# A selective scan in two tiles: one scan instruction over both, with a zero decay between them

## The chip, the cores and the metric

The kernel runs on one core of a Trainium2 chip. The metric is the device time of one execution in microseconds (us); lower is better. Engines are named as in the profile: PE is the matrix engine, DVE the vector engine, ACT the scalar engine, POOL GpSimd, and SP the engine that issues most plain DMAs.

## The reference

Eight samples of 256 channels and 1024 tokens pass through two layers. The first is a Mamba block: layer norm, a projection to 512 inner channels, a short causal convolution, a selective state-space scan, a gate, a projection back, and a feed-forward part. The second is full attention over the 1024 tokens with eight heads, followed by a mixture of experts of which two out of eight are used for each sample. Everything is fp32.

The part that the change touches is the scan. For each inner channel `d` and each of 16 states `s` it computes, token by token:

```python
dA = jnp.exp(dt_t[..., None] * A)
h = dA * h + (dt_t * x_t)[..., None] * B_t[:, None, :]
y = jnp.einsum('bds,bs->bd', h, C_t)
```

`h` begins at zero for each sample. There are 512 x 16 independent recurrences of 1024 tokens per sample.

## The kernel before

**Tiling.** The tokens of a sample are cut into two chunks of `CH` = 512. The 512 inner channels lie in four tiles of 128 partitions, taken in two halves of two tiles each (`NHALF` = 2). A step is one chunk, one state `s` and one half `h`: its tile `hb` has 128 partitions, two channel tiles `q` and 512 tokens. There are 16 chunks of 32 steps (`NSTEP`), so 512 steps. Steps with an even chunk number are those of a sample's first chunk; they start the recurrence from 0. Those with an odd number start from `state`, a small tile in which the last token of each row of the first chunk was put.

**One step.** Five functions, called by the loop over `now` near line 1606, make it up:

- `decay(g, q)` (line 568): one ACT exponential, `dt` times `-A`, into a 128x512 tile `da`, for tile `q`. `da` has four buffers, so that the decays of step `now + 2` are written where those of step `now` were read.
- `inputs(g)` (line 578): one DVE product, 128x1024, of `xd` with the broadcast row `B_t`, into `hb`.
- `scan(g, q)` (line 589): one DVE scan instruction per tile `q`, in place in `hb`. In the last call of a first chunk a POOL copy puts the last column of both tiles into `state`.
- `sums(g)` (line 604): one DVE product of `hb` with the row `C_t`, and a POOL DMA that adds the result to the accumulator of the chunk.
- `load_bc` (line 555): one SP DMA, 512 KB, which brings both rows of a state, broadcast over the partitions; it is used by the two halves.

**Order.** The order in the loop is scan 0, decay 0 of `now + 2`, scan 1, decay 1 of `now + 2`, `inputs` of `now + 1`, `sums` of `now`. The product of the next step thus stands between the scan and the sums that read it, and the sums stand between that product and the scan that reads it.

All other work is written as generators: `prologue` (norm, projection, convolution, `dt` for the next chunk), `gate_part`, `epilogue` (gate, projection, feed-forward of the chunk that has ended), `attention`, `project_part` and `experts`. A planner in the kernel (`Model`, `Queue`, `advance`, lines 62 to 119 and 1529 to 1549) keeps an estimate of when each engine is free. After each piece of a step it calls `advance`, which lets the generators issue their next instructions until the estimated time has caught up with DVE. A DVE instruction is charged as follows, and ACT and PE in a similar way:

```python
    def vec_cost(op, out, *_):
        return 0.16 + width(out) * (2.08e-3 if op == "tensor_tensor_scan" else 1.04e-3)
```

What the planner decides is only the order of the instructions on each engine; the synchronisation is by semaphores. An attention can begin when the `epilogue` of its sample's second chunk has ended, and its experts when the attention has been projected. After the last step, `while due: idle(0.25)` issues what is left.

Of the kernel before, what the change touches and what calls it, by code (L numbers as in the profile page):

```python
# [17 lines left out]
P = 128  # L18
# [36 lines left out]
def hybrid_kernel(ctx: ExitStack, tc: tile.TileContext, a: dict, out: bass.AP):  # L55
# [79 lines left out]
    def V(name, i=None, n=1):  # L135
        lo, hi = VEC[name]
        return vecs[:, lo:hi] if i is None else vecs[:, lo + i : lo + i + n]
# [297 lines left out]
    def prologue(i: int):  # L435
# [104 lines left out]
        for h in range(NHALF):  # L540
            dx = yield from mem.take(f"dx_{i}_{h}")
            dxs.append(dx)
            for r in range(2):
                act.activation(dx[:, r, :], xm[h][:, r, :], AF.Identity, scale=V("D", 2 * h + r))
        for h in range(NHALF):
            yield max(landed[h], model.end)
            vec.tensor_tensor(xm[h], xm[h], dts[h], ALU.mult)
        mem.end()
        me["acc", 0], me["acc", 1] = dxs
        me["xd"], me["dt"] = xm, dts  # L550


    das, bcs, hbs = {}, {}, {}

    def load_bc(n):
        i, s = divmod(n, NS)
# [6 lines left out]
    def place(g):  # L563
        i, k = divmod(g, NSTEP)
        s, h = divmod(k, NHALF)
        return i, s, h

    def decay(g, q):
        i, s, h = place(g)
        da = work_pool.tile([P, CH], F32, name=f"da_{g}_{q}", tag="da", bufs=4)  # L570
        n = (2 * h + q) * NS + s
        act.activation(da, chunk[i]["dt"][h][:, q, :], AF.Exp, scale=neg_a[:, n : n + 1])
        das[g, q] = (da, act.at)
        if q and s == NS - 1:
            model.end = act.at
            t4.put(chunk[i]["dt"][h])

    def inputs(g):

        i, s, h = place(g)  # L580
        hb = hbs[g] = h4.now(f"hb_{g}")
        bc, landed = bcs[g // NHALF]
        vec.at = max(vec.at, landed)
        xd = chunk[i]["xd"][h]
        vec.tensor_tensor(hb, xd, bc[:, 0, :].unsqueeze(1).to_broadcast([P, 2, CH]), ALU.mult)
        if s == NS - 1:
            t4.put(xd)

    def scan(g, q):

        i, s, h = place(g)
        c = i % NCH
        hb = hbs[g]
        d = 2 * h + q
        da, done = das.pop((g, q))
        vec.at = max(vec.at, done)
        vec.tensor_tensor_scan(
            hb[:, q, :], da, hb[:, q, :], 0.0 if c == 0 else state[:, s, d : d + 1],
            ALU.mult, ALU.add,
        )  # L600
        if q and c < NCH - 1:
            pool.tensor_copy(state[:, s, 2 * h : 2 * h + 2], hb[:, :, CH - 1])

    def sums(g):
# [891 lines left out]
    with tc.tile_pool(name="work", bufs=1) as work_pool:  # L1496

        def tagged(tag, n):
            return Slots(
                lambda nm, k: work_pool.tile([P, 2, CH], F32, name=nm, tag=f"{tag}_{k}"), n  # L1500
            )

        t4, h4, pt4 = tagged("t4", T4), tagged("h4", H4), tagged("pt", PT)
        for b in range(B):
            for m, nm in ((x1_d, "x1_d"), (t_d, "t_d"), (xf_d, "xf_d")):
                m[b] = dram.tile([NCH, P, KC, CH], F32, name=f"{nm}_{b}", tag=f"{nm}_{b}")

        class Scratch:


            def __init__(self, slots):
                self.slots, self.k, self.tile = slots, 0, work_pool.tile

            def keep(self, n, name, shape, dtype):
                return work_pool.tile(shape, dtype, name=name, tag=f"t4_{self.slots[n]}")

            def tmp(self, name, shape, dtype):
                self.k = (self.k + 1) % (len(self.slots) - 3)
                return self.keep(3 + self.k, name, shape, dtype)

        due, done = [], set()
        URGENT = {"a": 0, "p": 1, "g": 2, "e": 2, "o": 3, "s": 4, "x": 5, "y": 5}

        def start(stream, key, at=0.0):
            due.append([at, URGENT[key[0]], len(done) + len(due), stream, key])

        def advance():


            while True:
                model.t = min(model.t + TICK, vec.at)
                for d in sorted(due, key=lambda d: d[1:3]):
                    while d in due and d[0] <= model.t + 0.05:
                        if d[1] > 2 and max(pe.at, act.at) > model.t + LAG:
                            break
                        model.end = model.t
                        try:
                            at = next(d[3])  # L1540
                        except StopIteration:
                            due.remove(d)
                            done.add(d[4])
                            break
                        if at == POLL:
                            break
                        d[0] = (model.end if at is None else at) + 0.1
                if model.t >= vec.at:
                    break

        def idle(t):

            vec.at += t
            advance()

        def heads_and_projections():
            for b in range(B):
                while ("e", b * NCH + NCH - 1) not in done or ("s",) not in done:
                    yield POLL
                yield from attention(b)  # L1560

        def setup():
            mem = Owner(t4, 8)
            tiles = []
            for n in range(8):
                tiles.append((yield from mem.take(f"setup_{n}")))
            held = []
            for n in range(2):
                held.append((yield from pairs.take(f"setup_p{n}")))
            pl = Scratch([t4.of[id(t)][1] for t in tiles])  # L1570
            yield from fold(w1, HID // P, "ln2_g", "ln2_b", b1, "b1")
            yield
            yield from column_bias(pl)
            yield
            yield from bounds(pl)
            yield
            yield from values_bias(pl)
            expert_constants(pl)
            mem.put(*tiles)
            mem.end()  # L1580
            pairs.put(*held)

        def all_experts():
            for b in range(B):
                while not all(("o", b, c) in done for c in range(NCH)):
                    yield POLL
                yield from experts(b)

        first = prologue(0)
        next(first)  # L1590
        for t, src in loads:
            nc.sync.dma_start(t, src)
        run(fold(w_in, 2 * ND, "ln1_g", "ln1_b", b_in, "b_in"))
        start(first, ("p", 0))
        while ("p", 0) not in done:
            idle(0.25)
        start(heads_and_projections(), ("a",))
        start(all_experts(), ("x",))
        start(setup(), ("s",))
        nsteps = B * NCH * NSTEP  # L1600
        for n in range(AHEAD):
            load_bc(n)
        for n in range(4):
            decay(n // 2, n % 2)
        inputs(0)
        for now in range(nsteps):
            i, k = divmod(now, NSTEP)
            if k == FRONT and i + 1 < B * NCH:
                start(prologue(i + 1), ("p", i + 1), model.t)
            if k == GATE:  # L1610
                start(gate_part(i), ("g", i), model.t)
            n = now // NHALF + AHEAD
            if now % NHALF == 0 and n < B * NCH * NS:
                while "bc_d" not in chunk.get(n // NS, {}):
                    idle(0.5)
                load_bc(n)
            if now + 2 < nsteps:
                while "dt" not in chunk.get((now + 2) // NSTEP, {}):
                    idle(0.5)
            for q in range(2):  # L1620
                scan(now, q)
                advance()
                if now + 2 < nsteps:
                    decay(now + 2, q)
            if now + 1 < nsteps:
                while not h4.free:
                    idle(0.5)
                inputs(now + 1)
                advance()
            sums(now)  # L1630
            if k == NSTEP - 1:
                start(epilogue(i), ("e", i), model.t)
            advance()
        while due:
            idle(0.25)

        mx = work_pool.tile([P, 1], F32, name="mx", tag="s_mx")
        vec.tensor_reduce(mx, loads_e, AX.X, ALU.max)
        vec.tensor_scalar(mx, mx, capacity / L, None, ALU.is_gt)
        vec.tensor_tensor(bad, bad, mx, ALU.max)  # L1640
        vec.tensor_copy(flag, bad[0:1, :])
# [255 lines left out]
```

## Time and profile before

| | us |
|---|---|
| median of 3 runs | 3751.08 |
| lowest and highest | 3748.72, 3759.55 |
| profiled execution, its own time | 3752.05 |
| span of the profiled execution | 3750.2 |
| busy PE, DVE, ACT, POOL | 2954.9, 3127.6, 2519.5, 953.3 |
| first scan starts | 77.9 |
| last scan starts | 3297.4 |

The profile is one execution. A group of instructions is shown with its count, its busy time (overlaps counted once), its mean duration in ns, and the idle time of the engine just before it with what ended it. In a timeline a row has the start in us, the time that the merged instructions cover, and the engine; start minus start is what an instruction occupies when the next follows at once. A row of a table by stretches has the stretch, its length, and then the busy time and the count for PE, PEld (the weight loads), DVE, ACT and POOL, and at last the granted PE clock, the DMA share and GB/s. The mean granted PE clock of the execution is 0.882. All instructions but DMA issues are recorded by one helper, so that they carry one line number (L100) and are told apart by their tiles.

### The profile page before, as it was taken

The page shows a single profiled execution, that of the slowest core. Times are in us where ns is not written, and L with a number is a line of the kernel's source. Part 1 is how long each engine was busy: PE and PEld are TensorE (multiplying, and loading weights), DVE is VectorE, ACT ScalarE, POOL GpSimd, SP SyncE. Part 2 cuts the span into 40 slices and gives each one's busy share as a digit, 9 for nine tenths or more (in the row PEclk, how much of TensorE's full clock was granted, in tenths as well). Part 3 has the DMA queues.
Part 4 walks back from the last instruction along what each step waited for, and adds up shares of the span by engine and source line. Part 5 has one row for each costly group of instructions (what it writes and reads, how often), then busy time and mean ns, then how long its engine had stood idle before and what let it go on. Part 6 is the DMA issues. An engine that isn't in the chain of part 4 may idle for free. (4 is left out here: it accounts for less than half of the span.)

```text
span 3750.2 us, 33234 instructions
## 1 busy us (share of the span) xinstructions
PE 2954.9 (79%) x11155; PEld 1084.8 (29%) x11155; DVE 3127.6 (83%) x3322; ACT 2519.5 (67%) x3437; POOL 953.3 (25%) x1046
## 2 busy tenths in 40 slices
PE   4312636788788897988888987989898988999976
PEld 2101212322333223323233323332332323333322
DVE  4969999999899999997999899989999899932021
ACT  4333636687667876777868785877778795865644
POOL 0133123312341234322332223222322342211010
PEclk7655767899889998989899998989899999999988
DMA  4347787778687978887887878887878897832030
GB/s 113 69 92 175 161 176 173 169 164 176 159 205 164 207 159 191 199 195 163 179 194 164 196 169 186 196 181 175 191 174 179 200 204 170 200 84 82 34 76 21
DMA packets 178853, 596.84 MB, mean 159 GB/s; under 512 B 25184, under 2 KB 27872, under 8 KB 178672
## 3 DMA queue, kind: packets, MB, share of 16 engines
q0 software_dynamic: 103392, 364.44, 49.9%
q1 hardware_dynamic: 75280, 230.18, 19.0%
q8 instruction: 90, 1.47, 0.2%
q14 instruction: 91, 0.75, 0.1%
HBM read 234.36 MB, written 58.20 MB: 78 GB/s over the span
## 5 line engine op out<-in xcount | busy, mean ns | idle before, releaser
L100 ACT ACTIVATE da<-dt,neg_a 128x512 f32<-128x512 f32 x1024 | 721.2, 718 | 631.9 <-DVE hb L100 621.7
L95 POOL DMA_DIRECT2D dx<-hb x512 | 443.3, 867 | 1692.2 <-DVE hb L100 1440.8
L100 DVE TENSOR_TENSOR hb<-hb,bc 128x1024 f32<-128x1024 f32 x512 | 625.7, 1222 | 34.0 <-POOL state L100 20.2
L100 DVE TENSOR_TENSOR_SCAN hb<-da,state,hb 128x512 f32<-128x512 f32 x512 | 632.3, 1272 | 9.1 <-ACT da L100 9.1
L100 DVE TENSOR_TENSOR hb<-xm,bc 128x1024 f32<-128x1024 f32 x512 | 616.7, 1204 | 11.2 <-DMA dx<-hb 11.1
L100 DVE TENSOR_TENSOR_SCAN hb<-da,hb 128x512 f32<-128x512 f32 x512 | 603.9, 1211 | 1.0 <-ACT da L100 0.9
L100 ACT ACTIVATE pt<-sc 128x1024 f32<-128x1024 f32 x512 | 493.8, 1016 | 57.4 <-PE sc L100 57.1
L100 PE MATMUL sc<-qk,qk 32*128 32x512 f32 x2048 | 365.4, 665 | 57.9 <-ACT pt L100 43.2
L100 POOL COPY state<-hb 128x2 f32<-128x2 f32 x256 | 241.9, 945 | 454.8 <-DVE hb L100 450.9
L100 PE MATMUL num<-pt,v 128*32 128x512 f32 x2048 | 288.2, 632 | 46.4 <-DVE ot L100 46.4
L100 PE MATMUL facc<-fh,w 128*128 128x512 f32 x512 | 254.0, 647 | 35.0 <-ACT fh L100 22.2
L100 PE MATMUL den<-pt,ecb 128*32 128x512 f32 x2048 | 279.5, 614 | 0.0
L100 PE MATMUL fh<-x_f,w 128*128 128x512 f32 x480 | 239.2, 629 | 9.2 <-ACT fh L100 5.0
L100 PE MATMUL re<-he,g 128*128 128x512 f32 x472 | 223.1, 618 | 18.3 <-ACT he L100 10.1
L100 PE MATMUL he<-xe,g 128*128 128x512 f32 x448 | 221.1, 619 | 9.5 <-DVE fo L100 6.2
L100 ACT ACT_TABLE_LOAD x171 | 219.4, 1283 | 6.7 <-PE var_a L100 3.0
L100 PE MATMUL mo<-sz,w_out 128*128 128x512 f32 x256 | 125.6, 636 | 102.5 <-DVE sz L100 102.2
L100 PEld LDWEIGHTS sc<-qk,qk 32*128 32x128 f32 x2048 | 106.8, 188 | 290.8 <-ACT pt L100 114.0
L100 PE MATMUL z<-xz,w_in 128*128 128x512 f32 x256 | 130.0, 641 | 45.8 <-DMA xz<-xn_d 31.5
L100 PE MATMUL xin<-xn,w_in 128*128 128x512 f32 x256 | 134.6, 659 | 32.2 <-DVE xn L100 21.0
L100 PEld LDWEIGHTS facc<-fh,w 128*128 128x128 f32 x512 | 103.4, 208 | 186.6 <-issue 135.1
L100 DVE SCALAR_TENSOR_TENSOR xm<-xp,vecs,xm 128x512 f32<-128x512 f32 x192 | 143.4, 748 | 12.8 <-ACT xm L100 8.2
(320 smaller groups left out, 3922.7 us busy)
## 6 DMA issues: line engine op xcount, KB each, us to landing
dx<-hb POOLq DMA_DIRECT2D x512, 512.0 KB, 6.5
bc<-bc_d SPq DMA_DIRECT2D x256, 512.0 KB, 4.4
dt<-e POOLq DMA_DIRECT2D x32, 512.0 KB, 6.1
dt<-u POOLq DMA_DIRECT2D x32, 512.0 KB, 8.7
xe<-xf_d SPq DMA_DIRECT2D x28, 512.0 KB, 6.1
xn<-in_x SPq DMA_DIRECT2D x16, 512.0 KB, 6.2
xn_d<-xn SPq DMA_DIRECT2D x16, 512.0 KB, 2.8
xz<-xn_d SPq DMA_DIRECT2D x16, 512.0 KB, 8.6
```

Of the source, the lines that this page charges most:

```text
L95: f(*args, **kw)
L100: return f(*args, **kw)
```

## The change

The decays of a step are put into one tile of two rows, `das[n]`, allocated twice for even and odd steps. The first column of its second row is set to zero once and never written again, since the second exponential starts at column 1. One scan instruction runs over the 1024 elements of both rows. Where it passes into the second row, the zero decay drops what the first row left, so that the second row starts from its first input alone.

In a first chunk that is right as it stands. In a second chunk the second row has to start from its state, so the missing term, first decay times `state`, is added to the first input by a DVE instruction on one column, `carry`, between `inputs` and the scan. The decays of the first token are computed once per chunk and half in the prologue, 16 states at a time, into `first`. Both decays of step `now + 2` are now issued after the whole scan of step `now`, and `advance` is called once where it was called twice.

```diff
+        if c:
+            me["first"] = work_pool.tile([P, NHALF, NS], F32, name=f"first_{i}", tag="first", bufs=1)
         for h in range(NHALF):
             yield max(landed[h], model.end)
             vec.tensor_tensor(xm[h], xm[h], dts[h], ALU.mult)
+            if c:
+                n = (2 * h + 1) * NS
+                act.activation(
+                    me["first"][:, h, :], neg_a[:, n : n + NS], AF.Exp, scale=dts[h][:, 1, 0:1]
+                )
...
-    def decay(g, q):
+    def decays(g):
         i, s, h = place(g)
-        da = work_pool.tile([P, CH], F32, name=f"da_{g}_{q}", tag="da", bufs=4)
-        n = (2 * h + q) * NS + s
-        act.activation(da, chunk[i]["dt"][h][:, q, :], AF.Exp, scale=neg_a[:, n : n + 1])
-        das[g, q] = (da, act.at)
-        if q and s == NS - 1:
+        da = das[g % 2]
+        for q in range(2):
+            n = (2 * h + q) * NS + s
+            act.activation(
+                da[:, q, q:], chunk[i]["dt"][h][:, q, q:], AF.Exp, scale=neg_a[:, n : n + 1]
+            )
+        decayed[g] = act.at
+        if s == NS - 1:
...
+    def carry(g):
+        i, s, h = place(g)
+        if i % NCH:
+            u = hbs[g][:, 1, 0:1]
+            vec.scalar_tensor_tensor(
+                u, state[:, s, 2 * h + 1 : 2 * h + 2], chunk[i]["first"][:, h, s : s + 1], u,
+                ALU.mult, ALU.add,
+            )
+
+    def scan(g):
...
+        vec.at = max(vec.at, decayed.pop(g))
+        row = hb.rearrange("p q t -> p (q t)")
         vec.tensor_tensor_scan(
-            hb[:, q, :], da, hb[:, q, :], 0.0 if c == 0 else state[:, s, d : d + 1],
-            ALU.mult, ALU.add,
+            row, das[g % 2].rearrange("p q t -> p (q t)"), row,
+            0.0 if c == 0 else state[:, s, 2 * h : 2 * h + 1], ALU.mult, ALU.add,
         )
...
+        das = [work_pool.tile([P, 2, CH], F32, name=f"da_{n}", tag=f"da_{n}") for n in range(2)]
...
-        for n in range(4):
-            decay(n // 2, n % 2)
+        for n in range(2):
+            vec.memset(das[n][:, 1, 0:1], 0.0)
+            decays(n)
...
-            for q in range(2):
-                scan(now, q)
-                advance()
-                if now + 2 < nsteps:
-                    decay(now + 2, q)
+            scan(now)
+            advance()
+            if now + 2 < nsteps:
+                decays(now + 2)
             if now + 1 < nsteps:
                 while not h4.free:
                     idle(0.5)
                 inputs(now + 1)
+                carry(now + 1)
                 advance()
             sums(now)
```

More of the change, by code (lines that the diff above doesn't have):

```diff
@@ L550, in prologue @@
         me["xd"], me["dt"] = xm, dts
-    das, bcs, hbs = {}, {}, {}
+    decayed, bcs, hbs = {}, {}, {}
     def load_bc(n):
@@ L587, in inputs @@
             t4.put(xd)
-    def scan(g, q):
+    def carry(g):
[7 more added lines that the diff above has]
+    def scan(g):
         i, s, h = place(g)
@@ L593, in scan @@
         hb = hbs[g]
-        d = 2 * h + q
-        da, done = das.pop((g, q))
-        vec.at = max(vec.at, done)
+        vec.at = max(vec.at, decayed.pop(g))
+        row = hb.rearrange("p q t -> p (q t)")
         vec.tensor_tensor_scan(
-            hb[:, q, :], da, hb[:, q, :], 0.0 if c == 0 else state[:, s, d : d + 1],
-            ALU.mult, ALU.add,
+            row, das[g % 2].rearrange("p q t -> p (q t)"), row,
+            0.0 if c == 0 else state[:, s, 2 * h : 2 * h + 1], ALU.mult, ALU.add,
         )
-        if q and c < NCH - 1:
+        if c < NCH - 1:
             pool.tensor_copy(state[:, s, 2 * h : 2 * h + 2], hb[:, :, CH - 1])
```

## The prediction

> **What bounds the kernel now.** I read the page first, then the groups of VectorE (DVE), its timeline step by step, the waits, and last the busy time of the stretch after the scans.
>
> Busy shares (part 1) and the 40 slices (part 2):
>
> ```profile
> PE 2954.9 (79%) x11155; PEld 1084.8 (29%) x11155; DVE 3127.6 (83%) x3322; ACT 2519.5 (67%) x3437; POOL 953.3 (25%) x1046
> ...
> PE   4312636788788897988888987989898988999976
> ...
> DVE  4969999999899999997999899989999899932021
> ```
>
> DVE holds slices 2 to 35 at 9 with a few dips. Then it falls to almost nothing, and PE runs at 9 until near the end. So there are two regimes: scans until 3299 us (the last scan), bound by DVE, and 451 us afterwards, bound by PE and by the dependent chain of the last sample. The two kinds of scan, and the waits between ScalarE (ACT) and DVE over the decays:
>
> ```profile
> L100 DVE TENSOR_TENSOR_SCAN hb<-da,state,hb 128x512 f32<-128x512 f32 x512 | 632.3, 1272 | 9.1 <-ACT da L100 9.1
> L100 DVE TENSOR_TENSOR_SCAN hb<-da,hb 128x512 f32<-128x512 f32 x512 | 603.9, 1211 | 1.0 <-ACT da L100 0.9
> ```
>
> ```profile
> ACT da L100 <- DVE hb L100: 621.7, 430, 9.4
> ...
> DVE hb L100 <- ACT da L100: 10.0, 8, 3.3
> ```
>
> A scan with a state pointer costs 0.06 us more than one with a constant start. ACT runs ahead of DVE: 430 times it stood at a decay until DVE had freed the buffer; the reverse happened 8 times.
>
> The mean durations are not what a step costs, because DVE instructions overlap. The timeline of DVE shows it by its starts (columns: start, union of the merged instructions):
>
> ```profile
> 3188.27 2.45 DVE L100 TENSOR_TENSOR_SCAN hb<-da,state,hb 128x512 f32<-128x512 f32 x2
> 3190.64 1.20 DVE L100 TENSOR_TENSOR hb<-xm,bc 128x1024 f32<-128x1024 f32 x1
> 3191.75 1.22 DVE L100 TENSOR_TENSOR hb<-hb,bc 128x1024 f32<-128x1024 f32 x1
> 3192.89 2.45 DVE L100 TENSOR_TENSOR_SCAN hb<-da,state,hb 128x512 f32<-128x512 f32 x2
> ```
>
> The product that takes 1.20 us is followed after 1.11 us: an instruction that does not need its forerunner starts 0.08 us before that one ends. A pair of scans occupies 3190.64 - 3188.27 = 2.37 us. Three other places give the prices that the change needs:
>
> ```profile
> 142.58 0.68 DVE L100 SCALAR_TENSOR_TENSOR val<-cnt,io_ch 128x512 f32<-128x512 f32 x1
> 143.29 1.02 DVE L100 TENSOR_REDUCE last<-val 128x32 f32<-128x512 f32 x1
> 144.24 2.31 DVE L100 SCALAR_TENSOR_TENSOR xm<-xp,vecs,xm 128x512 f32<-128x512 f32 x3
> 146.46 4.49 DVE L100 TENSOR_TENSOR oh<-hl,io_ch 128x2048 bf16<-128x2048 f32 x2
> 150.87 0.75 DVE L100 SCALAR_TENSOR_TENSOR xm<-xp,vecs,xm 128x512 f32<-128x512 f32 x1
> ```
>
> ```profile
> 1000.52 0.23 DVE L100 TENSOR_SCALAR obias<-obias,w2e 128x2 f32<-128x2 f32 x1
> 1000.66 2.33 DVE L100 TENSOR_TENSOR_SCAN hb<-da,hb 128x512 f32<-128x512 f32 x2
> 1002.91 1.20 DVE L100 TENSOR_TENSOR hb<-xm,bc 128x1024 f32<-128x1024 f32 x1
> ```
>
> The reduce reads `val` and starts 0.03 us after its end (142.58 + 0.68 = 143.26), not 0.08 before: reading one's forerunner costs about 0.12 us. A 2048-wide product takes (150.87 - 146.46) / 2 = 2.20 us. A tiny instruction with a pointer scalar takes 0.14 us (1000.52 to 1000.66). A pair of constant-start scans takes 2.25 us.
>
> [...] 512 scanned elements last 1211 ns, a 1024-wide product 1204 to 1222. So one 1024-wide scan should occupy what the 2048-wide product does. [...]
>
> **The change part by part.** There are 512 steps, 256 in first chunks (constant start) and 256 in second chunks (state pointer).
>
> - Merged scans. First chunk: 2.25 - 2.20 = 0.05 us saved. Second chunk: 2.37 - (2.20 + 0.06) = 0.11 us. Sum 12.8 + 28.2 = 41 us less DVE.
> - The carry, 256 times, stands directly behind the input product that it reads, and in the order of the built program its wait is on DVE itself. It makes that product cost its full latency (+0.12) and takes 0.14 itself: 0.26 x 256 = 67 us more. Behind it stand the sums of the step before, which do not read it, so no second stall; the scan comes after those. No row has a 1-wide pointer form of exactly this kind; between 0.07 (a tiny form without pointer) and 0.23 (no overlap behind it), plus 0.12, the bounds are 49 and 90 us. I take 67.
> - So DVE gains work: 67 - 41 = +26 us, about +0.15 us in each second-chunk step and -0.05 in each first-chunk step.
> - Decays. Same 1024 activations, 512 of them one element shorter. Both now wait for the whole scan, where the first waited for half of it, and both must be done before the next use. The second decay ends up to 0.72 us later. Counted over the timelines of ACT and DVE, in 15 of the 512 steps the second decay was not done when its pair's first scan began; adding up those shortfalls gives 14 us, and 26 if everything is 0.7 us later, against 10 us waited now. I take +8 (0 to +16). POOL's `state` copies stay 256 and keep their place behind the scan; SP's queue is untouched.
> - `first`: 16 activations of 16 columns, [...]two at a time in the prologue, hidden because ACT idles 622 us at the decays[...]. Two `memset`s: nothing that shows.
> - What moves. The planner charges a scan 2.08 ns per element and 0.16 per instruction, so it thinks each first-chunk step 0.16 us shorter and packs less other work beside the scans. In the built order, 100 of the attention's `pt` exponentials follow the last decay on ACT instead of 90, with 2 or 3 more `he` banks, 2 `re` banks, one `wo`. At the rates of the stretch 3452 to 3616 (sc, num, den together 3.3 us for two `pt`; `he` 2.0, `re` 3.7, `wo` 1.9), that is 16.5 + 5 + 7.4 + 1.9 = 31 us of PE that now comes after the scans. There PE has no room:
>
> ```profile
> 3299.00:3452.00 153.00, 145.34 (x544) 57.50 (x536) 41.62 (x83) 79.69 (x102) 14.64 (x17) 0.99 0.31 77
> 3452.00:3616.00 164.00, 162.22 (x898) 51.58 (x895) 15.67 (x23) 106.72 (x119) 8.21 (x9) 1.00 0.18 47
> 3616.00:3751.00 135.00, 84.92 (x188) 33.18 (x186) 33.20 (x75) 50.12 (x65) 12.39 (x13) 0.82 0.13 40
> ```
>
>  (Columns: length, then busy PE, PEld, DVE, ACT.) PE is 95% and 99% busy in the first two, but idle for 50 of the last 135 us, and the new order puts some `he` and `re` of sample 6 there. I take half: +15 (0 to +31).
>
> Sum: in the scans, DVE waits already for other things some 6% of the time, so I let a fifth of 26 + 8 - 2 (three DVE operations moved behind the scans) vanish: +25. With the tail's +15: +40 on the profiled 3752.05 us (span 3750.2), thus 3792; the shown median is 1 us lower: **3791**. A measurement of this kernel can tell about 0.3%, 11 us, from no change.
>
> **Rivals.**
> - Only the DVE sum arrives; the attention of sample 7 has to wait for its own layer anyway, and the backlog fills PE's gaps: 3751 + 20 = 3771 (3763 to 3776). For it: the idle 50 us. Against: 99% in the stretch before. Chance 0.19.
> - It cancels: DVE's idle takes the carries in and the tail takes the backlog, 3751 to 3762. Chance 0.13.
> - ACT becomes a partner in the bound: decays late in many steps, exponentials late behind them, PE later; 0.72 us in one step of ten is 37 us more, 3810 to 3830. Against: the 622 us ACT idles. Chance 0.13.
> - Faster: the carry starts without the stall and costs 0.14 or less. With 36 us for carries DVE gains 5 us of time, and at 0.07 us each it gains 23; if all of that reaches the end, and the tail takes no more than now, 3728 to 3746, say 3735. The sign turns at 41 / 256 = 0.16 us per carry. Against: the 0.12 us stall is seen wherever an instruction reads its forerunner. Chance 0.06.
> - The merge does not do what it says (a 1024-wide scan slower than two of 512): no reason seen; inside the heavy case.
>
> **How the numbers follow.** Main case 0.49 (3777 to 3808), with those above: slower 0.49 + 0.19 + 0.13 = 0.81, same 0.13, faster 0.06. The range 3758 to 3818 leaves out the faster case, part of the cancelled one and the far half of the heavy one.
>
> **What would show it.** DVE rows: scans 128x1024 x512, mean near 2.27 us (constant) and 2.34 (pointer); a carry group x256 near 0.22 us. In the timeline of a second chunk, product to carry 1.23 us, carry to sums 0.14, whole steps 4.77 instead of 4.62; in a first chunk 0.05 shorter. The last scan near 3325, and more than 451 us behind it. It is wrong if the carry follows the product after 1.11 us, if the wide scans start less than 2.1 us apart, or if the last scan ends before 3299.

## Result, and the profile after

| | before | after |
|---|---|---|
| median of 6 runs, us | 3753.89 | 3766.82 |
| lowest and highest | 3748.72, 3759.55 | 3763.82, 3774.25 |
| profiled execution, its own time | 3752.05 | 3766.41 |
| span of the profiled execution | 3750.2 | 3764.6 |
| last scan ends | 3298.7 | 3272.8 |
| span behind the last scan | 451.5 | 491.8 |

The changed kernel takes 1.0036 times as long, 95% interval 1.0022 to 1.0050: 13 us slower. The forecast was 3791, that is 40 us slower. The direction was right and the size three times too large. The table shows already that the two parts moved in opposite ways: the scans ended *earlier*, and the stretch behind them grew. The last three rows are of one profiled execution of each kernel; executions of one kernel differ by some 10 us.

First the page of the changed kernel, the busy shares and two rows of the slices:

```profile
PE 2970.2 (79%) x11155; PEld 1089.9 (29%) x11155; DVE 3139.2 (83%) x3068; ACT 2501.5 (66%) x3451; POOL 930.2 (25%) x1046
...
PE   4312627798888896999898987898889889999986
...
DVE  3979999999999999989999999999999979812121
```

DVE is 11.6 us busier (3127.6 before), with 254 fewer instructions. Its row of slices has fewer dips than before, and it falls a little earlier: slices 35 and 36 (counted from 1) hold 8 and 1, where before they held 9 and 3. The groups of DVE in the changed kernel (busy, mean ns, idle ahead):

```profile
L100 DVE TENSOR_TENSOR_SCAN hb<-da,state,hb 128x1024 f32<-128x1024 f32 x256 | 600.6, 2346 | 11.5 <-ACT da L100 11.5
L100 DVE TENSOR_TENSOR_SCAN hb<-da,hb 128x1024 f32<-128x1024 f32 x256 | 584.6, 2284 | 2.4 <-ACT da L100 2.3
...
L100 DVE SCALAR_TENSOR_TENSOR hb<-state,first,hb 128x1 f32<-128x1 f32 x256 | 56.2, 219 | 9.1
```

Three prices stand here as they were forecast: 2.28 and 2.35 us for the scans (2.27 and 2.34), 0.22 for the carry. The 9.1 us of idle ahead of the carries, with no releaser named, are 256 gaps of 35 ns (9.1 / 256). The 16 activations of `first` took 291 to 308 ns each:

```profile
L100 ACT ACTIVATE first<-neg_a,dt x16: 291/296/308, 196.4 to 3083.8; 128x16 f32<-128x16 f32 x16
```

The timeline of DVE, one step of a second chunk:

```profile
3199.96 2.34 DVE L100 TENSOR_TENSOR_SCAN hb<-da,state,hb 128x1024 f32<-128x1024 f32 x1
3202.22 1.20 DVE L100 TENSOR_TENSOR hb<-xm,bc 128x1024 f32<-128x1024 f32 x1
3203.46 0.22 DVE L100 SCALAR_TENSOR_TENSOR hb<-state,first,hb 128x1 f32<-128x1 f32 x1
3203.60 1.22 DVE L100 TENSOR_TENSOR hb<-hb,bc 128x1024 f32<-128x1024 f32 x1
3204.73 2.34 DVE L100 TENSOR_TENSOR_SCAN hb<-da,state,hb 128x1024 f32<-128x1024 f32 x1
```

Start to start: the scan occupies 2.26, the product ahead of the carry 1.24 (it was 1.11), the carry 0.14, the sums 1.13. The step takes 3204.73 - 3199.96 = 4.77 us, which is the forecast figure. The waits for the decays, from the table of waits:

```profile
ACT da L100 <- DVE hb L100: 552.4, 252, 12.3
...
DVE hb L100 <- ACT da L100: 13.8, 10, 4.2
```

ACT stands less often (252 times against 430), since a pair of decays now waits once. DVE stands 3.8 us longer. And the stretches behind the last scan (columns as before: length, then busy PE, PEld, DVE, ACT, POOL, and the PE clock, DMA share, GB/s):

```profile
3273.00:3449.00 176.00, 172.03 (x692) 66.66 (x682) 35.70 (x44) 97.42 (x119) 13.71 (x15) 1.00 0.28 65
3449.00:3616.00 167.00, 160.33 (x873) 49.27 (x874) 20.18 (x60) 97.08 (x112) 13.44 (x14) 0.96 0.17 48
3616.00:3765.00 149.00, 97.69 (x217) 39.77 (x215) 37.41 (x80) 62.09 (x79) 15.13 (x16) 0.84 0.19 50
```

PE is busy for 430 us of these 492; before, it was 392 of 452. So 38 us of PE work came behind the scans, the stretch is 40 longer, and PE idles there for 62 us as against 60. The free PE time at the end, which the forecast let take half of the displaced work, took none of it in this order.

### The profile page after: what moved, and what is told of

Read it like the earlier page. It is cut to its first block, busy times and chain, and to the rows that moved or that the text cites. A ratio compares the mean times of both kernels' runs of the same rounds, so it can differ in the third digit from the quotient of the medians.

```text
span 3764.6 us, 32994 instructions
## 1 busy us (share of the span) xinstructions
PE 2970.2 (79%) x11155; PEld 1089.9 (29%) x11155; DVE 3139.2 (83%) x3068; ACT 2501.5 (66%) x3451; POOL 930.2 (25%) x1046
## 4 chain that ended last, share of the span: by engine, by line
DVE 47%; PE 20%; issue 11%; ACT 9%; DMA 8%; POOL 4%; DVEq 0%; POOLq 0%; SPq 0%; ACTq 0%
DVE hb L100 34%; DMA dx<-hb 6%; DVE xm L100 3%; POOL state L100 3%; PE sc L100 2%; PE re L100 2%; PE num L100 2%; ACT L100 2%; PE fh L100 2%; PE he L100 2%; PE den L100 2%; PE facc L100 2%; ACT da L100 1%; ACT fh L100 1%; PE halves L100 1%
## 5 line engine op out<-in xcount | busy, mean ns | idle before, releaser
L100 ACT ACTIVATE da<-dt,neg_a 128x512 f32<-128x512 f32 (+1 forms) x1024 | 680.5, 714 | 560.7 <-DVE hb L100 552.4
L100 DVE TENSOR_TENSOR_SCAN hb<-da,state,hb 128x1024 f32<-128x1024 f32 x256 | 600.6, 2346 | 11.5 <-ACT da L100 11.5
L100 DVE TENSOR_TENSOR_SCAN hb<-da,hb 128x1024 f32<-128x1024 f32 x256 | 584.6, 2284 | 2.4 <-ACT da L100 2.3
L100 POOL COPY state<-hb 128x2 f32<-128x2 f32 x256 | 222.0, 867 | 354.3 <-DVE hb L100 345.4
L100 PE MATMUL den<-pt,ecb 128*32 128x512 f32 x2048 | 288.5, 632 | 0.0
```

Of the source, the lines that this page charges most:

```text
L100: return f(*args, **kw)
```

## Experiments

All runs in one table; ratios are to the kernel before, run on the same chip. *Scans* is the part of the profiled execution from the start of the first scan to the end of the last, called the scan phase below; *idle* is DVE's idle time in it, and *behind* is the time from the end of the last scan to the end of the span. These three are of one execution, which can lie 10 us off its kernel's median (`oldorder` 3758 against 3769, `joint` 3737 against 3727), so differences of a few us between them say nothing.

| kernel | median us | ratio [95%] | scans | idle | behind |
|---|---|---|---|---|---|
| before | 3754 | 1 | 3220.8 | 206.6 | 451.5 |
| after | 3766.8 | 1.0036 [1.0022, 1.0050] | 3193.3 | 170.3 | 491.8 |
| neworder | 3731.5 | 0.9938 [0.9921, 0.9954] | 3163.3 | 156.3 | 484.7 |
| oldorder | 3768.8 | 1.0039 [1.0025, 1.0053] | 3223.3 | 199.1 | 454.2 |
| nocarry | 3712.4 | 0.9883 [0.9866, 0.9899] | 3149.0 | 181.2 | 485.3 |
| nostall | 3859.6 | 1.0277 [1.0260, 1.0294] | 3291.9 | 286.4 | 487.9 |
| joint | 3727.4 | 0.9931 [0.9912, 0.9950] | 3184.6 | 175.3 | 471.1 |
| charge | 3777.5 | 1.0059 [1.0037, 1.0082] | 3226.0 | 212.3 | 472.1 |
| charge_all | 3789.5 | 1.0100 [1.0080, 1.0120] | 3224.4 | 215.4 | 482.4 |
| latedecay | 3726.7 | 0.9934 [0.9913, 0.9955] | 3159.3 | 152.1 | 485.0 |
| decays_last | 3758.8 | 1.0014 [1.0005, 1.0022] | 3233.5 | 216.1 | 445.4 |
| decays_first | 3798.1 | 1.0126 [1.0109, 1.0143] | 3240.2 | 229.4 | 485.9 |
| decays_later | 3740.3 | 0.9970 [0.9958, 0.9981] | 3218.0 | 204.1 | 435.3 |
| firstonly | 3730.6 | 0.9950 [0.9932, 0.9967] | 3196.1 | 202.0 | 453.8 |
| before_n1 | 3756.3 | 1.0008 [0.9999, 1.0017] | 3214.8 | 201.8 | 466.1 |
| before_n2 | 3780.4 | 1.0077 [1.0051, 1.0102] | 3226.6 | 214.4 | 473.9 |
| joint_n1 | 3744.8 | 0.9979 [0.9972, 0.9987] | 3213.5 | 207.1 | 457.4 |
| joint_n2 | 3748.4 | 0.9980 [0.9972, 0.9988] | 3205.2 | 200.5 | 464.9 |
| after_n1 | 3752.8 | 1.0005 [0.9991, 1.0018] | 3203.1 | 177.9 | 463.7 |
| after_n2 | 3765.9 | 1.0041 [1.0028, 1.0054] | 3196.7 | 175.5 | 490.3 |

### Instructions apart from order: neworder, oldorder, nocarry, nostall

`neworder` has the instructions of the kernel before in the order of the changed one, and the planner is charged as there: apart from the scans, the decays, the carries and `first`, the sequences of PE, ACT, DVE and POOL are the same in both traces.

```diff
+        if q == 0:
+            model.do(vec, 0.16 + 2 * CH * 2.08e-3)
+        nc.vector.tensor_tensor_scan(
...
                 scan(now, q)
-                advance()
-                if now + 2 < nsteps:
+            advance()
+            if now + 2 < nsteps:
+                for q in range(2):
                     decay(now + 2, q)
...
                 inputs(now + 1)
+                if (now + 1) // NSTEP % NCH:
+                    model.do(vec, 0.16 + 1.04e-3)
```

> The old instructions (two scans of 512 a step, four decay buffers, no carry) in exactly the order that the changed kernel has for all other work; the planner is charged as in the changed kernel. Theory A (what a step costs DVE and what the order does simply add): scan phase 3193 - 23 = 3170 us, about 490 us behind it as in the changed kernel, total 3744 (ratio 0.997). Theory B (other engines set the length of the scan phase, DVE's idle takes in what the carry costs): scan phase 3193, behind it 490, total 3767 (1.0035). Theory C (the longer stretch behind the scans came from the new instructions, not from the order): 451 us behind the scans, total below 3730 or about 3754.

`oldorder` is the reverse: the merged scan and the carry, with the charges and the calls of `advance` where the kernel before has them. It can't keep the place between the two scans: the merged scan stands where the first one stood, and both decays where the second did.

```diff
 # the decays, against the changed kernel
+        if q == 0:
+            return
         for q in range(2):
...
 # the scan, against the kernel before
-        vec.tensor_tensor_scan(
-            hb[:, q, :], da, hb[:, q, :], 0.0 if c == 0 else state[:, s, d : d + 1],
...
+        model.do(vec, 0.16 + CH * 2.08e-3)
+        if q == 0:
+            row = hb.rearrange("p q t -> p (q t)")
+            nc.vector.tensor_tensor_scan(
+                row, das[g % 2].rearrange("p q t -> p (q t)"), row,
+                0.0 if c == 0 else state[:, s, 2 * h : 2 * h + 1], ALU.mult, ALU.add,
+            )
```

> The new instructions (one scan of 1024, carry, first) in exactly the order that the kernel before has for all other work. Theory A: scan phase 3221 + 23 = 3244, behind it 451, total 3777 (ratio 1.006). Theory B: scan phase 3221, behind it 451, total 3754 (1.000). Theory C: behind the scans 490, total 3790 or more.

`nocarry` is the changed kernel with the carry's charge but not its instruction.

```diff
-            vec.scalar_tensor_tensor(
-                u, state[:, s, 2 * h + 1 : 2 * h + 2], chunk[i]["first"][:, h, s : s + 1], u,
-                ALU.mult, ALU.add,
-            )
+            model.do(vec, 0.16 + 1.04e-3)
```

> The changed kernel without the carry instruction (the second tile of each half starts a second chunk from zero), its charge in the planner kept, so that all other instructions stand in the same order. DVE is relieved of 256 x 0.257 = 66 us. Theory A: scan phase 3193 - 66 = 3127, behind it 490, total 3700 (0.986). Theory B: no more than 10 us less, 3757 or more (1.001). Half of the 66: 3734.

`nostall` makes the inputs a step earlier, so that a scan and a sum lie between the product and the carry that reads it. The planner's charge keeps its old place.

```diff
-                inputs(now + 1)
+                charge(now + 1)
                 carry(now + 1)
+                if now + 2 < nsteps:
+                    inputs(now + 2)
                 advance()
```

> The changed kernel with the input product issued one step earlier on DVE, so that a whole scan stands between it and the carry that reads it; all else in the same order. The carry then costs 0.14 instead of 0.26, 256 x 0.12 = 30 us less of DVE. Theory A: scan phase 3163, total 3737 (0.9955), below the kernel before. Theory B: 3760 to 3767. If the earlier product waits for the DMA that empties its buffer (landing 6.5 us, margin now 8 instead of 12.6 us), some of the 30 us come back as waits on dx<-hb.

**What the first three show.** Read the scan phase in the table as work plus idle. The stretches of the scan phase, rounded to whole us, show DVE's busy time as the third entry behind the length. They are, in this order, of the kernel before, `neworder`, `nocarry` and the changed kernel:

```profile
78.00:3299.00 3221.00, 2523.29 (x9431) 920.67 (x9435) 3014.33 (x3100) 2247.94 (x3101) 913.59 (x996) 0.88 0.76 174
```

```profile
80.00:3243.00 3163.00, 2470.65 (x9275) 903.28 (x9279) 3006.75 (x3096) 2225.68 (x3075) 893.15 (x989) 0.88 0.78 177
```

```profile
80.00:3229.00 3149.00, 2473.81 (x9271) 904.90 (x9271) 2967.72 (x2585) 2209.66 (x3091) 894.22 (x989) 0.88 0.78 178
```

```profile
79.00:3273.00 3194.00, 2499.94 (x9279) 911.92 (x9283) 3023.60 (x2842) 2209.87 (x3092) 883.56 (x989) 0.87 0.77 175
```

- From `neworder` to `nocarry` the scans are merged, and with them the waits of the decays: DVE's work in the scan phase falls from 3163.3 - 156.3 = 3007.0 to 3149.0 - 181.2 = 2967.8, by 39 us. The forecast was 41. But DVE's idle time grows by 25 at the same time, and the medians differ by 19 us: about half of what was saved did not reach the end.
- From `nocarry` to after only the carry comes in: ratios 0.9883 and 1.0036, 57 us for 256 carries (forecast 67). In the scan phase DVE's work grows by 55 and the carry gaps add 9, while its other idle time falls.
- From `neworder` to after both: work plus the 9 us of carry gaps is +25 us (3023.0 - 3007.0 + 9.1; forecast +26). The ratios say +0.98%, 37 us. In the old order, `oldorder` against before, they say +0.39%, 15 us. The mean of both is 26. The first comparison is the cleaner one; the second holds the moved places named above, too.
- The order alone is worth -0.62% with the old instructions (`neworder`), and nothing with the new ones (1.0036 against 1.0039). In both cases it shortens the scan phase (by 57 us from before to `neworder`, by 30 from `oldorder` to after) and lengthens what is behind (by 33 and 38).

Each of the three medians lies nearer to what theory A expected (what a step costs and what the order does add up) than to theory B.

The merging at its best, with nothing between the products, is in the timeline of `nocarry`; the product is followed after 1.13 us and not 1.24:

```profile
3102.10 1.22 DVE L100 TENSOR_TENSOR hb<-xm,bc 128x1024 f32<-128x1024 f32 x1
3103.23 1.22 DVE L100 TENSOR_TENSOR hb<-hb,bc 128x1024 f32<-128x1024 f32 x1
3104.37 2.34 DVE L100 TENSOR_TENSOR_SCAN hb<-da,state,hb 128x1024 f32<-128x1024 f32 x1
```

`nostall` took the carry away from the product that it reads, and lost more elsewhere. DVE's work in the scan phase is 17.5 us less (3023.0 to 3291.9 - 286.4 = 3005.5). In the changed kernel the sums start 83 ns before the carry ahead of them ends (median); if the 256 carries of `nostall` overlap what stands ahead of them as much, that is 21 us, an estimate that fits. But it costs 93 us more than the changed kernel (3859.6 - 3766.8): the product, made one step earlier, waits for the accumulating DMA that still reads its tile (median from issue to landing 6.5 us). From its table of waits (L597 is the product of `inputs`):

```profile
DVE hb L597 <- DMA dx<-hb: 162.9, 95, 6.9
```

In the changed kernel that wait is 8.5 us, 4 times. So a product made a whole step earlier is too early for the four `hb` buffers there are, and what the stall costs at the end of the kernel wasn't measured. Other places for the carry were not tried.

### Which part of the order: joint, charge, charge_all, latedecay

`joint` is the kernel before with one `advance` for both scans, and both decays behind it; charges as before.

```diff
                 scan(now, q)
-                advance()
-                if now + 2 < nsteps:
+            advance()
+            if now + 2 < nsteps:
+                for q in range(2):
                     decay(now + 2, q)
```

> The kernel before with one edit: both scans of a step in a row, then one advance, then both decays; charges as before. Theory J (what made the new order faster is that scans and decays stand together): 3735 or less. Theory K (it is the 0.16 us less that the planner charges for a first-chunk step): no change, 3750 to 3760. Theory N (any change of order moves the time by some 20 us either way, without a trend): anywhere from 3730 to 3775.

`charge` is the kernel before whose planner takes the first chunk's second scan to be 0.16 us shorter, as the changed kernel's does; `charge_all` does it in every step.

```diff
-        vec.tensor_tensor_scan(
+        model.do(vec, CH * 2.08e-3 + (0.0 if q and c == 0 else 0.16))
+        nc.vector.tensor_tensor_scan(
```

> The kernel before with one edit: in first-chunk steps the planner charges the second scan 0.16 us less, as it does for the merged scan; the instructions and the places of scans and decays stay. Theory K: 3732, with 480 to 490 us behind the last scan. Theory J: 3755. Theory N: anywhere from 3730 to 3775.

> The kernel before, the planner charging every step 0.16 us less, in second chunks too. Theory K: the scan phase shortens further (below 3163), the stretch behind it grows further (above 490), total 3715 to 3730. Theory J: 3755. Theory N: anywhere from 3730 to 3775.

`latedecay` is `neworder` with the second tile's decay issued ahead of the first's, so that both wait for both scans, as in the changed kernel.

```diff
-        n = (2 * h + q) * NS + s
...
+        for q in (1, 0):
+            n = (2 * h + q) * NS + s
```

> The run neworder (old instructions in the changed kernel's order) with one edit: of the two decays of a step the second tile's is issued first, so that on ACT both wait for the whole pair of scans, as both decays do behind the merged scan. nocarry against neworder gained 19 us where 43 us of scan occupancy were taken away. Theory L (24 us of it are lost because the decays start only when the whole scan has ended): 3731 + 24 = 3755, with DVE waits on da of 20 us or more. Otherwise: 3731.

**The charge** alone costs 0.59% and puts 21 us more behind the scans, with the scan phase no shorter (+5); with twice as many steps charged so, it is 1.00% and 31 us. None of the expectations went above 3775, and the two ran in 3777 and 3790. This looks like the displaced work of the forecast, but it isn't shown: a reordering that means nothing (`before_n2`, below) costs 0.77% and puts 22 us more behind. **The grouping** alone (`joint`) brings 0.69%, and its scan phase is 36 us shorter although no instruction in it got cheaper: DVE's idle time in it is 31 us less. And **late decays** cost nothing: `latedecay` and `neworder` agree (0.9934, 0.9938), and ACT's wait is the same in both. The first fence is `neworder`, the second `latedecay`:

```profile
ACT da L575 <- DVE hb L603: 468.2, 400, 12.1
```

```profile
ACT da L578 <- DVE hb L607: 466.3, 404, 12.1
```

### Why the grouping helps: decays_last, decays_first, decays_later, firstonly

A theory was at hand (P): while ACT stands at a decay that waits for DVE, the exponentials and copies issued behind it wait too. Its rival (Q) was that the two scans standing together are what counts. Before, ACT stood 622 us at decays; in `joint` 477. Three places of the decays test it, each against `joint`:

```diff
 # decays_last: two advances, both decays behind the second
                 scan(now, q)
-            advance()
+                advance()
             if now + 2 < nsteps:
```

> The kernel before with one edit: after each of the two scans an advance as before, but both decays only after the second advance. Theory P (the gain of joint, 26 us, comes from the decays standing behind the other work in ACT's queue, so that ACT works instead of standing at a decay): 3725 to 3738, ACT's wait at da 480 us instead of 622. Theory Q (it comes from the two scans standing together on DVE): 3750 to 3760.

```diff
 # decays_first: decays ahead of the one advance
-            advance()
             if now + 2 < nsteps:
                 for q in range(2):
                     decay(now + 2, q)
+            advance()
```

> The kernel joint with one edit: both decays ahead of the advance, directly behind the two scans. Theory P: slower than the kernel before, 3770 or more, ACT's wait at da above 650 us. Theory Q: 3727, as joint.

```diff
 # decays_later: decays behind the advance of the inputs
             advance()
-            if now + 2 < nsteps:
-                for q in range(2):
-                    decay(now + 2, q)
...
                 advance()
+            if now + 2 < nsteps:
+                for q in range(2):
+                    decay(now + 2, q)
             sums(now)
```

> The kernel joint with one edit: the decays behind the input product of the next step and its advance. Theory P: ACT's wait at da falls below 400 us; the time is 3715 to 3727, unless the decays are now late for their scans (DVE's wait on da 30 us or more instead of 8.5). Theory Q: 3727.

```diff
 # firstonly: the merged scan in first chunks alone, so no carry is needed
+        if c:
+            nc.vector.tensor_tensor_scan(
+                hb[:, q, :], da[:, q, :], hb[:, q, :], state[:, s, d : d + 1], ALU.mult, ALU.add
+            )
+        elif q:
+            row = hb.rearrange("p q t -> p (q t)")
+            nc.vector.tensor_tensor_scan(
+                row, da.rearrange("p q t -> p (q t)"), row, 0.0, ALU.mult, ALU.add
+            )
```

> The kernel joint with the merged scan in first chunks only, where no carry is needed (second chunks keep two scans with the state pointer; the zero column is set again at each first chunk). DVE is relieved of 256 x 0.054 = 14 us less 14 tiny memsets. If it all arrives: 3713. If half arrives, as nocarry against neworder: 3720. If nothing: 3727.

At the bad end the theory fits: with the decays ahead of `advance`, ACT stands longest and the kernel is the slowest of the three (1.0126, where Q expected no loss). From the waits of `decays_first`, and then of `joint`:

```profile
ACT da L100 <- DVE hb L100: 731.5, 599, 11.6
```

```profile
ACT da L100 <- DVE hb L100: 477.4, 416, 12.1
```

At the good end it isn't shown. In `decays_last` ACT stands only 502 us, nearly as little as in `joint`, and the kernel is no faster than before (1.0014), which is what Q expected. DVE's waits for ACT in the scan phase did fall, from 68.8 us to 39.1, but those for PE rose from 32.8 to 70.7. In `decays_later` ACT stands 386 us, the least of all, and the gain is 0.3%, less than that of `joint`. But there the decays come late: DVE waits 35.7 us for them. The first fence is `decays_later`, the second `joint`:

```profile
DVE hb L100 <- ACT da L100: 35.7, 14, 7.6
```

```profile
DVE hb L100 <- ACT da L100: 8.5, 5, 4.3
```

So in these orders ACT's standing alone doesn't set the time. Each place was tried in one order only, and by the next section one order is worth up to 0.8%; of the three only `decays_first` lies clearly further from `joint` than that (2.0%). `firstonly` should have gained 13 us over `joint` from its 256 merged scans; it gained nothing (0.9950 and 0.9931, intervals overlapping); this, too, is one order.

### How much is chance of the order: six null reorderings

The planner's list changes whenever an estimate moves, even by one thousandth of a microsecond. `before_n1`, `joint_n1` and `after_n1` have the first edit, `before_n2`, `joint_n2` and `after_n2` the second. No instruction is changed; only the order of other work is.

```diff
 # n1
-        return 0.16 + width(out) * (2.08e-3 if op == "tensor_tensor_scan" else 1.04e-3)
+        return 0.161 + width(out) * (2.08e-3 if op == "tensor_tensor_scan" else 1.04e-3)
 # n2
-        return 2.6 if op.startswith("preload") else 0.36 + width(out) * 0.68e-3
+        return 2.6 if op.startswith("preload") else 0.361 + width(out) * 0.68e-3
```

> The kernel before, the planner's charge per DVE instruction 0.161 instead of 0.160 us; no instruction is changed, only the order of the other work. Theory S (the order's share belongs to the loop): 3750 to 3760. Theory N (scatter): anywhere from 3730 to 3775.

> The kernel before, the planner's charge per ACT instruction 0.361 instead of 0.360 us. Theory S: 3750 to 3760. Theory N: anywhere from 3730 to 3775.

> The kernel joint, the planner's charge per DVE instruction 0.161 instead of 0.160 us. Theory S: 3722 to 3735. Theory N: anywhere from 3715 to 3765.

> The kernel joint, the planner's charge per ACT instruction 0.361 instead of 0.360 us. Theory S: 3722 to 3735. Theory N: anywhere from 3715 to 3765.

> The changed kernel, the planner's charge per DVE instruction 0.161 instead of 0.160 us; only the order of the other work differs. Theory S (the order's share belongs to the loop): 3760 to 3774. Theory N (scatter): anywhere from 3745 to 3800; a value near 3790, the forecast, would mean that the forecast's error lies within what a reordering does.

> The changed kernel, the planner's charge per ACT instruction 0.361 instead of 0.360 us. Theory S: 3760 to 3774. Theory N: anywhere from 3745 to 3800.

These runs carry the study's main caution. One kernel in three such orders: before 1, 1.0008, 1.0077; after 1.0036, 1.0005, 1.0041; `joint` 0.9931, 0.9979, 0.9980. A change of the order that means nothing moves the time by up to 0.8%, 29 us, and the interval of that run (1.0051 to 1.0102) shows that the difference is real for that order. The expectation that the time belongs to the loop and not to the order failed in four of the six (`before_n2`, both of `joint`, `after_n1`). Over the three orders the means are 1.0028 (before), 1.0027 (after) and 0.9963 (`joint`).

The two parts of the span scatter differently. The scan phase of the changed kernel is shorter in all three orders (3193 to 3203 us) than that of the kernel before in any of its three (3215 to 3227): means 3197.7 and 3220.7, so 23 us shorter. What lies behind varies from 464 to 492 us in the first and from 452 to 474 in the second: means 481.9 and 463.8, so 18 us longer. `joint` has 3201.1 and 464.5: it shortens the scans by 20 us at no cost behind. Of the +40 us behind the scans in the first comparison 18 are thus left in the means: the kernel before has its shortest stretch in its own order (451.5 against 466.1 and 473.9), and the changed kernel has 463.7 once. PE's work behind the scans goes the same way: 38 us more in the first comparison, 17 in the means (423 and 407).

With the old instructions there are now five orders of each kind. Two scans with a decay after each: 1, 1.0008, 1.0059, 1.0077, 1.0100. Both scans, one `advance`, both decays: 0.9931, 0.9934, 0.9938, 0.9979, 0.9980. They don't overlap, though some of the five are near relatives and two of the first kind have changed charges. The means are 1.0049 and 0.9952; for the three pairs that differ in the grouping alone the gap is 0.65%. The changed kernel, which has the second grouping, stands at a mean of 1.0027: 0.75%, 28 us, above the second kind, which is again about what its instructions should cost (+26).

## Why the prediction was right or wrong

**Right: the price of the instructions.** Merged scans -41 us of DVE: -39 measured in DVE's work. Carry +67 us: 57 measured at the end. The stall of 0.12 us behind the product was taken from one reduce in the trace of before, and the trace of after bears it out: the 256 carries, which wait for the product that they read, start 35 ns after its end (median), where the 227 sums that directly follow a carry, and read nothing of it, start 83 ns before its end. Together that makes the same 0.12 us. Net DVE +26: +25 in the trace at equal order, and about 26 us in the mean of the two comparisons at the end. This is why the kernel did not get faster. That the first comparison came out slower also took these particular orders: over three orders each, the means of before and after are equal.

**Wrong: the part "What moves".** This is the step that failed. It treated the new order as nothing but displaced work: +15 us in the tail, and -2 us of relief in the scan phase. Both terms were mis-sized, the relief above all. With the old instructions (before to `neworder`) the new order shortens the scan phase by 57 us and lengthens the tail by 33; with the new ones (`oldorder` to after) by 30 and 38. At the end that is -0.62% and nothing, where the forecast had +13 us. Of the 57 us (3220.8 to 3163.3), 7 are DVE work moved out and 50 are waits that went away: by their releasers, DVE's waits in the scan phase fell from 68.8 to 45.2 us for ACT, from 52.0 to 30.8 for DMA, and hardly for PE and POOL. So the scan phase of the changed kernel, forecast at +25, is at -27.5, and at -23 in the mean of three orders. The count of the displaced work (31 us of PE) lies between the 38 of this order and the 17 of the means; the tail of +15 was too small for this order (+40: PE's idle time at the end took nothing), and near the mean (+18). The forecast also looked for the cause in the charge of 0.16 us, whose effect (`charge`, +0.59%) can't be told from the scatter of the order. The gain goes with the grouping of scans and decays, which the forecast priced only as a risk.

**Wrong, small: the late decays.** +8 us forecast; DVE's waits for them rose by 3.8 us, and `latedecay` shows no cost at the end.

**Wrong: one place to look.** The last scan was to end near 3325, and the forecast called itself wrong if it ended before 3299. It ended at 3272.8. With the step at its forecast 4.77 us, that mark pointed away from the instructions; the runs at equal instructions showed that it was the order.

**The rivals.** "Only the DVE sum" names a range that holds the result (3763 to 3776), but not its reason: the tail did take the backlog in full. The ACT partner did not appear: ACT stands 552 us at the decays, so it had time. "Faster" fell with the stall it denied. "It cancels" missed the first comparison (3751 to 3762 against 3767), but it is what the means over three orders say, and half its reason appeared: DVE's idle time in the scan phase fell from 206.6 to 170.3 us while its work grew.

**The range** (3758 to 3818) held the result near its lower end, in part by luck: the order did far more to both parts than was allowed for (-57 to -30 us in the scan phase, +33 to +38 behind it, against -2 and at most +31), but the errors cancel in good part. It was built from bounds of costs; no part of it stood for the scatter of the order, which is 0.8% on its own and as large as the whole net effect of the instructions.

**What stays open.** Why one grouping is better than the other was not settled: ACT's standing time fits the bad end, and at the good end neither theory is shown. How much of the miss belongs to the grouping and how much to this one order can't be told from three orders. Since in their means before and after are equal (1.0028, 1.0027), the 13 us themselves are within what another order of the same instructions makes.

**Better than both.** `joint` (3727), `latedecay` (3727) and `neworder` (3731) beat both kernels. All keep the separate scans and change only the order. In its two null reorderings `joint` still gains 0.2%; how much of the other 0.5% is one order's luck can't be told from three.

## What to carry to other kernels

Before merging instructions, compare what is saved (here 0.05 and 0.11 us per pair) with what the repair costs: one dependent instruction on a single column cost here 0.22 us (`nocarry` against after, 57 us for 256) to 0.26 us (0.14 + 0.12 in the timeline), as much as two to five merges. When a planner decides the order, build the old instructions in the new order and the new ones in the old before explaining a difference, and reorder by a meaningless amount a few times to learn how much an order is worth by itself. Work pushed behind the critical phase is not only a loss there: ask at the same time which waits it took out of the phase.

## What the runs showed of the hardware

The carry, a DVE instruction on one column that reads its forerunner, occupied the engine in the changed kernel for 0.14 us of its own and made its forerunner cost 0.12 us more: it started 35 ns after the forerunner's end (median of 256), where the sums behind it, which don't read it, started 83 ns before its end. Saved DVE time was not saved kernel time, though DVE is at 9 of 10 in most slices: of 39 us less work in `nocarry` than in `neworder` 25 came back as idle time in the scan phase, and 19 us reached the end. And the `hb` tiles were tight: in `nostall`, which writes one a step earlier, the products waited 95 times, 1.7 us on average (162.9 us), for DMAs that cost them 8.5 us in the changed kernel.
